# Latent attention block: VectorE and ScalarE in program order in blocks 1 to 3, with new buffer pools, piece places and load order

## The chip, the cores and the metric

The kernel runs on one core of a Trainium2 chip. The time is the device time of one execution in microseconds (us); the median of several executions is given. Lower is better.

## The reference

One transformer block on 2048 tokens of width 512, batch 1: latent attention with 16 heads, a residual and a layer norm, then one linear layer, a residual and a second layer norm.

```python
cq  = rms_norm(x @ w_qa.T, q_a_ln_w)                  # query latents, width 384
q   = cq @ w_qb.T                                     # 16 heads of 128 + 64
ckv = x @ w_kva.T                                     # width 128 + 64
ckv_l = rms_norm(ckv[..., :128], kv_a_ln_w)
kv  = ckv_l @ w_kvb.T                                 # 16 heads of 128 (keys) + 128 (values)
# rotary embedding on the 64-wide parts of q and of ckv
scores = einsum('bhqd,bhkd->bhqk', q_full, k_full) * 192 ** -0.5
scores = where(causal, -inf, scores)
out = softmax(scores) @ v                             # per head
x = layernorm(x + out @ w_o.T)
x = layernorm(x + x @ (w * scale_weight[:, None]).T + bias)
```

The result must be close to float32, so most operands are kept as a high and a low half, and each product is made of three products of halves.

## The kernel before

The key projection is folded into the query weights and the value projection into the output weights, so that all heads share one set of keys (`Kn`, `Kp`) and values (`V`). The 2048 queries are cut into four blocks `b` of 512. A block runs over eight pairs `p` of heads, a pair over four query tiles `qt` of 128 rows, and from block 1 on each tile over its two heads `j`. One such (b, p, qt, j) is called a head here; blocks 1 to 3 have 64 each. It has `nk` = (4b + qt + 1) x 128 keys: 640 to 1024 in block 1, 1152 to 1536 in block 2, 1664 to 2048 in block 3. Block 0 handles both heads of a tile at once, interleaved with the projections of the inputs and the weights. After block 3 a tail multiplies by the output weights, adds, normalizes and runs the linear layer (L763 onward is its layer norm, L786 its largest product).

The work on one head, in the order in which the program emits it:

- `head_scores`: TensorE writes the scores into PSUM (L408), in one piece `s` up to 1024 keys and in two beyond. There are three score buffers in blocks 1 and 3; block 2 has two for the first piece and two smaller ones for the second. VectorE adds the causal mask to the last 128 keys (L414; in block 3 for j = 0, TensorE does it at L410), and takes the maximum of each piece (L441). Between the two pieces' maxima the generator of the head before is advanced. A small operation makes the exponential's bias (L448 for one piece, L450 for two). The rest of the head before follows. ScalarE then takes the exponential into `pr` (L456), with its sum, and VectorE inverts the sum (L466 or L468, then L469).
- `head_probs`, a generator that is run while the next head is being emitted: ScalarE writes the scaled probabilities as float16 into `hl` (L477), VectorE writes what float16 left over (L480), both in two cuts from 1152 keys on; then one DMA transposes `hl` into the ring `PT` (L484), issued from SP.
- `values`: TensorE multiplies the transposed probabilities of a pair of heads by `V` (L533), in two halves that are run some heads later (`run_values`, with a lag of three query tiles in blocks 1 and 2 and two in block 3); ScalarE copies the result to `ot` (L538), and it goes to memory.
- `fill` advances the projections for the next pair or block by one piece of nine matmuls, at the heads whose number 2 qt + j is listed in `at`. `project_nope` has two pieces, each followed by L66 on ScalarE and L67 on VectorE. `project_pe`, once in two pairs, has two pieces as well, each followed by two L339 on VectorE; after the second, GpSimd combines the products (L346, L347), ScalarE rounds them (L349), and GpSimd spreads them (L360, L361).

The order of TensorE and of SP is the program's own in blocks 1 to 3 (`manual_schedule`). VectorE, ScalarE and GpSimd are ordered by a scheduler that works from its own estimate of durations. All pools of blocks 1 to 3 are one pool `blk13` with two buffers for each of `pr` and `hl`, and the ring lies in it. `load_wq` and `load_block`, called at the end of the last pair's query projection, put the loads of the next block's query weights `wq`, of its query latents `cq` (1.5 MB) and of its rotary tables `cs` on SP's queue.

Of the kernel before, what the change touches and what calls it, by code (L numbers as in the profile page):

```python
# [9 lines left out]
F16 = mybir.dt.float16  # L10
BF16 = mybir.dt.bfloat16
F32 = mybir.dt.float32
# [7 lines left out]
P = 128  # L20
# [5 lines left out]
NB = 4  # L26
QB = 512
NPAIR = H // 2
# [21 lines left out]
def mla_block(ctx: ExitStack, tc: tile.TileContext, a, out):  # L50
# [6 lines left out]
    def move(queue, dst, src):  # L57
        queue.dma_start(dst.bitcast(F32), src.bitcast(F32))

    def split(ps, h, l, scale=None):  # L60

        if scale is None:
            nc.scalar.activation(h, ps, AF.Copy)  # L63
            nc.vector.tensor_tensor(l, ps, h.bitcast(F32), ALU.subtract)  # L64
        else:
            nc.scalar.activation(h, ps, AF.Copy, scale=scale)  # L66
            nc.vector.scalar_tensor_tensor(l, ps, scale, h.bitcast(F32), ALU.mult, ALU.subtract)  # L67
# [42 lines left out]
    blk = ctx.enter_context(tc.tile_pool(name="blk", bufs=2, side="right"))  # L110
# [177 lines left out]
    def put_in(all=False):  # L288
        kept = []
        for n, dst, src in later:  # L290
            if n == 0 or all:
                nc.sync.dma_start(dst, src)
            else:
                kept.append([n - 1, dst, src])
        later[:] = kept

    def load_block(b):
        if b == NB:
            return
        cq = prj.tile([P, 2, LT, QB], F32R, tag="cq", name=f"cq{b}")  # L300
        if b:
            move(state["queue"], cq, cq_d[b])
        cs = prj.tile([P, 2, QB], F32, tag="cs", name=f"cs{b}")
        (state["queue"] if b else nc.sync).dma_start(cs, a["csq"][b])
        state["cq"], state["cs"] = cq, cs
# [3 lines left out]
    def load_wq(b, p):  # L309
        if b == NB:  # L310
            return
        w = state["wq", b, p] = prj.tile([P, 2, LT, 256], F32R, tag="wq", name=f"wq{b}_{p}")
        c0 = (p % 2) * 256
        move(state["queue"], w, wq_d[p // 2][:, :, :, c0 : c0 + 256])
# [52 lines left out]
    def project_nope(b, p, direct=None):  # L367
        if direct is None and ("wq", b, p) not in state:
            load_wq(b, p)
        w = state.pop(("wq", b, p)) if direct is None else direct  # L370
        cq = state["cq"]
        qn = blk.tile([P, 2, 2, QB], F32R, tag="qn", name=f"qn{b}_{p}")
        for j in range(2):
            ps = psum["m"].tile([P, QB], F32, tag="m", name=f"ps_qn{b}_{p}_{j}")
            n = 0
            for lt in range(LT):
                for i, k in ((0, 0), (0, 1), (1, 0)):
                    nc.tensor.matmul(  # L378
                        ps, w[:, i, lt, j * P : (j + 1) * P], cq[:, k, lt, :], start=n == 0, stop=n == 8
                    )  # L380
                    n += 1
            split(ps, qn[:, 0, j, :], qn[:, 1, j, :], kvln)
            if j == 1:
                state["qn", b, p] = qn
                if b or p == NPAIR - 1:
                    load_wq(*((b, p + 1) if p + 1 < NPAIR else (b + 1, 0)))
                if p == NPAIR - 1:
                    load_block(b + 1)
            yield

    def project(b, p):
# [27 lines left out]
    def head_scores(pool, b, p, j, qt, nk, prev):  # L419
        t = 4 * b + qt  # L420
        r = rq[:, t : t + 1]
        cks = chunks(nk)
        nt = len(cks)
        neg = small.tile([P, 2], F32, tag="neg", name="neg")
        tiles = []
        for ti, ck in enumerate(cks):

            if b == 2 and ti == 1:
                ps = psum["t"].tile([P, 1, 512], F32, tag="t", name=f"s{b}_{p}_{qt}_{j}_{ti}", bufs=2)
            else:  # L430
                ps = psum["s"].tile(
                    [P, 2, 512], F32, tag="s", name=f"s{b}_{p}_{qt}_{j}_{ti}", bufs=2 if b == 2 else 3
                )
            w = ck[0][1]
            for ci, (c0, w) in enumerate(ck):
                d = nk - P - c0
                score(ps[:, ci, :], c0, w, b, p, j, qt, d if 0 <= d < w else None)
            v = ps[:, : len(ck), :w]
            if ti == nt - 1 == 0:
                next(prev, None)  # L440
            nc.vector.tensor_reduce(neg[:, ti : ti + 1], v, axis=AX.XY, op=ALU.max, negate=True)  # L441
            tiles.append((v, ck[0][0], len(ck), w))
            if ti < nt - 1:
                next(prev, None)
                next(prev, None)
        bias = small.tile([P, 1], F32, tag="bias", name="bias")
        if nt == 1:
            nc.vector.tensor_scalar(bias, neg[:, 0:1], r, None, ALU.mult)  # L448
        else:
            nc.vector.tensor_scalar(bias, neg[:, 0:1], neg[:, 1:2], r, ALU.min, ALU.mult)  # L450
        for _ in prev:
            pass
        pr = pool.tile([P, nk], F32, tag="pr", name=f"pr{b}_{p}_{qt}_{j}")
        sums = small.tile([P, 2], F32, tag="sums", name="sums")
        for ti, (v, c0, n, w) in enumerate(tiles):
            nc.scalar.activation(  # L456
                pr[:, c0 : c0 + n * w].rearrange("p (a c) -> p a c", a=n),
                v,
                AF.Exp,
                bias=bias,  # L460
                scale=r,
                accum_out=sums[:, ti : ti + 1],
            )
        inv = small.tile([P, 1], F32, tag="inv", name="inv")
        if nt == 1:
            nc.vector.tensor_scalar(inv, sums[:, 0:1], 1.0 / P_UP, None, ALU.mult)  # L466
        else:
            nc.vector.tensor_scalar(inv, sums[:, 0:1], sums[:, 1:2], 1.0 / P_UP, ALU.add, ALU.mult)  # L468
        nc.vector.reciprocal(inv, inv)  # L469
        return pr, inv  # L470

    def head_probs(pool, b, p, j, qt, nk, PT, pr, inv):
        hl = pool.tile([P, 2, nk], F16, tag="hl", name=f"hl{b}_{p}_{qt}_{j}")
        step = nk if nk <= 1024 else nk // 2
        cuts = [slice(c, c + step) for c in range(0, nk, step)]
        for c in cuts:
            nc.scalar.activation(hl[:, 0, c], pr[:, c], AF.Copy, scale=inv)  # L477
        yield
        for c in cuts:
            nc.vector.scalar_tensor_tensor(hl[:, 1, c], pr[:, c], inv, hl[:, 0, c], ALU.mult, ALU.subtract)  # L480
            if c != cuts[-1]:
                yield
        n2 = 2 * nk
        nc.sync.dma_start_transpose(  # L484
            PT[:, j * n2 : (j + 1) * n2].rearrange("p (k q) -> p k q", q=P), hl.rearrange("p a c -> p (a c)")
        )
        put_in()
# [64 lines left out]
    def drain():  # L552
        while fillers:
            fill()
# [48 lines left out]
    def flush():  # L603
        while probs:
            for _ in probs.pop():
                pass

    def units(pool, ring, b):
        lag = min(ring.shape[1] // (2048 * (b + 1)) - 1, 3)

        for p in range(NPAIR):
# [1 line left out]


            if p + 1 == NPAIR:
                at = (1, 2, 4, 5) if b < NB - 1 else (1, 3, 5, 7)
            elif p % 2 == 0 and p + 2 < NPAIR:
                at = (0, 1, 2, 3) if (b, p) == (1, 0) else (0, 1, 3, 4)
            else:
                at = (3, 4)  # L620
            if b and p % 2 == 0 and p + 2 < NPAIR:
                fillers.append(project_pe(b, p // 2 + 1))
            if p + 1 < NPAIR:
# [24 lines left out]
            for qt in range(4):  # L648
                nk = (4 * b + qt + 1) * P
# [28 lines left out]
                        run_values(lag)  # L678
                vals.append([vg, 0, s0, s0 + 4 * nk])
            drain()  # L680

    def half_values():
        next(vals[0][0])
# [37 lines left out]

    ctx_m = ctx.enter_context(ExitStack())
    psum["m"] = ctx_m.enter_context(tc.tile_pool(name="ps_m", bufs=2, space=PSUM, side="right", reuse_waits="tile"))
    blk13 = ctx_m.enter_context(tc.tile_pool(name="blk13", bufs=2, reuse_waits="tile"))
    ring = blk13.tile([P, 12 * 2048], F16, name="ring", bufs=1)
    side[:] = []
    state["queue"] = nc.sync
    with tc.manual_schedule(engines={mybir.EngineType.PE, mybir.EngineType.SP}):
        for b in range(1, NB):
            with ExitStack() as ctx_s:  # L730
                for k in ("t", "s") if b == 2 else "s":
                    psum[k] = ctx_s.enter_context(
                        tc.tile_pool(name=f"ps_{k}{b}", bufs=1, space=PSUM, reuse_waits="tile")
                    )
                units(blk13, ring, b)
        put_in(True)
    state["queue"] = nc.gpsimd
    pcr, wvo, wv, wo = (state[k] for k in ("pcr", "wvo", "wv", "wo"))
# [89 lines left out]
            if late and next(late[0], None) is None:  # L828
                late.pop(0)

    ET = mybir.EngineType
    CUT = 2
    with tc.manual_schedule(engines={ET.PE}):
        order = [(b, p) for b in range(NB) for p in range(NPAIR)]
# [93 lines left out]
```

## Time and profile before

| | us |
|---|---|
| median of 3 executions (1647.24 to 1654.08) | 1650.19 |
| the profiled execution | 1647.43 |
| its span | 1645.3 |
| block 0, with all projections of the inputs (to the first scores of block 1) | 257.5 |
| block 1, 64 heads | 254.0 |
| block 2, 64 heads | 360.9 |
| block 3, 64 heads | 501.6 |
| last values and tail | 271 |

The profile's names: PE is TensorE's matmuls and PEld its weight loads, DVE is VectorE, ACT ScalarE, POOL GpSimd, SP the engine that issues most DMAs. A group's row gives line, engine, operation, what it writes and reads, the shape, its count, busy time, the mean duration of one, and, behind the last bar, the idle time of the engine before it and what ended that. In the order of time a row begins with its start and duration in us, and a bracket gives the idle time of that engine before it and the releaser. A row of windows gives the stretch, its length, the busy time and count of each engine, the granted clock of TensorE as a share of full speed, the busy share of the DMA engines and GB/s.

Waits that the other sections refer to, from the list of waits (engine and line that waited, what it waited for; total us, times, longest): VectorE's inv (L468) for the exponential (L456) 78.2, 64, 2.4; ScalarE's exponential for the bias (L450) 110.6, 69, 5.6; ScalarE's L477 for the transposing DMA 69.8, 40, 6.8; TensorE's scores for the exponential 26.5, 25, 3.6; TensorE's L334 for the query latents 4.5, 2, 3.1.

### The profile page before, as it was taken

The page shows a single profiled execution, that of the slowest core. Times are in us where ns is not written, and L with a number is a line of the kernel's source. Part 1 is how long each engine was busy: PE and PEld are TensorE (multiplying, and loading weights), DVE is VectorE, ACT ScalarE, POOL GpSimd, SP SyncE. Part 2 cuts the span into 40 slices and gives each one's busy share as a digit, 9 for nine tenths or more (in the row PEclk, how much of TensorE's full clock was granted, in tenths as well). Part 3 has the DMA queues.
Part 4 walks back from the last instruction along what each step waited for, and adds up shares of the span by engine and source line. Part 5 has one row for each costly group of instructions (what it writes and reads, how often), then busy time and mean ns, then how long its engine had stood idle before and what let it go on. Part 6 is the DMA issues. An engine that isn't in the chain of part 4 may idle for free. (4 is left out here: it accounts for less than half of the span.)

```text
span 1645.3 us, 24717 instructions
## 1 busy us (share of the span) xinstructions
PE 1563.1 (95%) x9130; PEld 1295.0 (79%) x9130; DVE 1162.4 (71%) x2099; ACT 928.4 (56%) x1631; POOL 361.7 (22%) x436
## 2 busy tenths in 40 slices
PE   8898999999999999999999999999998997999997
PEld 7787877888777888888887787787786785788876
DVE  5778678787768888888786777777776673555564
ACT  4777766665646676667665666666665563311120
POOL 2342426045016213050053103103100000022132
PEclk9999999999999999999999999999999999999999
DMA  6889666888888888788986787786788788333230
GB/s 208 237 225 236 174 179 159 153 170 170 148 188 172 163 171 166 152 167 159 201 168 144 141 162 139 155 161 126 149 161 175 161 173 187 104 115 120 98 109 32
DMA packets 632839, 262.48 MB, mean 160 GB/s; under 512 B 570288, under 2 KB 611120, under 8 KB 631696
## 3 DMA queue, kind: packets, MB, share of 16 engines
q1 hardware_dynamic: 621184, 233.35, 66.2%
q0 software_dynamic: 4768, 17.99, 3.5%
q10 hardware_dynamic: 6768, 9.57, 2.1%
q8 instruction: 72, 1.18, 0.3%
q14 instruction: 47, 0.39, 0.1%
HBM read 83.17 MB, written 35.13 MB: 72 GB/s over the span
## 5 line engine op out<-in xcount | busy, mean ns | idle before, releaser
L408 PE MATMUL s<-Kn,qn 128*128 128x512 f32 (+4 forms) x1920 | 524.6, 379 | 28.4 <-ACT pr L456 26.5
L533 PE MATMUL o<-ring,V 128*128 128x256 f16 x3252 | 397.0, 275 | 19.4 <-DMA ring<-hl 14.8
L456 ACT ACTIVATE pr<-s,bias,rq 128x1024 f32<-128x1024 f32 (+3 forms) x320 | 324.1, 1016 | 150.8 <-DVE bias L450 110.6
L408 PEld LDWEIGHTS s<-Kn,qn 128*128 128x128 f32 x1920 | 339.7, 191 | 82.6 <-ACT pr L456 38.7
L480 DVE SCALAR_TENSOR_TENSOR hl<-pr,inv,hl 128x1024 f16<-128x1024 f32 (+7 forms) x320 | 357.2, 1137 | 66.1 <-ACT hl L477 64.6
L477 ACT ACTIVATE hl<-pr,inv 128x1024 f16<-128x1024 f32 (+7 forms) x320 | 295.4, 961 | 172.5 <-DMA ring<-hl 69.8
L533 PEld LDWEIGHTS <-V 128*128 128x128 f16 x3264 | 304.4, 98 | 101.2 <-issue 54.6
L441 DVE TENSOR_REDUCE neg<-s 128x1 f32<-128x1024 f32 (+3 forms) x320 | 318.6, 996 | 75.4 <-PE s L408 71.0
L408 PE MATMUL s<-Kp,pe 128*128 128x512 f32 (+4 forms) x1280 | 363.0, 365 | 0.0
L408 PEld LDWEIGHTS s<-Kp,pe 128*128 128x128 f32 x1280 | 235.3, 190 | 29.8
L346 POOL TENSOR_TENSOR prod<-prod 128x512 f32<-128x512 f32 x15 | 19.2, 1283 | 666.6 <-DVE prod L339 666.6
L378 PE MATMUL ps_qn<-cq,wq 128*128 128x512 f32 x576 | 145.9, 398 | 0.7 <-ACT ot L538 0.3
L361 POOL TENSOR_TENSOR pe<-prod,ph 32x512 fp32r<-32x512 f32 x92 | 141.6, 1539 | 11.0 <-issue 5.1
L786 PE MATMUL acc<-wvo,oh 128*128 128x512 f32 x448 | 143.5, 401 | 0.0
L378 PEld LDWEIGHTS ps_qn<-cq,wq 128*128 128x128 f32 x576 | 107.9, 191 | 22.1 <-ACT ot L538 0.8
L786 PEld LDWEIGHTS acc<-wvo,oh 128*128 128x128 f32 x448 | 83.4, 188 | 20.9 <-issue 2.9
L284 POOL DMA_DIRECT2D ot_d<-ot x33 | 18.8, 568 | 319.2 <-ACT ot L538 292.3
L786 PE MATMUL acc<-wvo,ol 128*128 128x512 f32 x224 | 88.4, 394 | 0.0
L468 DVE TENSOR_SCALAR inv<-sums 128x1 f32<-128x1 f32 x128 | 26.9, 210 | 78.3 <-ACT pr L456 78.2
L538 ACT ACTIVATE ot<-o 128x256 f32<-128x256 f32 x128 | 48.0, 376 | 59.9 <-PE o L533 59.9
L334 PE MATMUL ps_pe<-cq,wpe 128*128 128x512 f32 x288 | 71.9, 395 | 5.6 <-DMA cq<-cq_d 4.5
L66 ACT ACTIVATE qn<-ps_qn,kvln 128x512 fp32r<-128x512 f32 x64 | 43.7, 684 | 51.1 <-PE ps_qn L378 51.0
(140 smaller groups left out, 1608.8 us busy)
## 6 DMA issues: line engine op xcount, KB each, us to landing
wq<-wq_d SPq DMA_DIRECT2D x22, 768.0 KB, 5.7
o<-ot_d SPq DMA_DIRECT2D x32, 512.0 KB, 3.3
ot_d<-ot SPq DMA_DIRECT2D x95, 128.0 KB, 2.6
wpe<-wpe_d SPq DMA_DIRECT2D x10, 768.0 KB, 5.3
wq<-wq_d POOLq DMA_DIRECT2D x9, 768.0 KB, 6.4
wq_d<-wst SPq DMA_DIRECT2D x9, 512.0 KB, 4.4
cq_d<-cqst SPq DMA_DIRECT2D x18, 256.0 KB, 3.8
ot_d<-ot POOLq DMA_DIRECT2D x33, 128.0 KB, 3.2
```

The lines of the kernel that those rows point to most:

```text
L66: nc.scalar.activation(h, ps, AF.Copy, scale=scale)
L334: nc.tensor.matmul(ps, w[:, i, lt, x * P : (x + 1) * P], cq[:, k, lt, :], start=n == 0, stop=n == 8)
L361: (nc.gpsimd if not quick or (b, g) == (0, 0) and j % 2 else nc.vector).tensor_tensor(pe[64 + 32 * x : 96 + 32 * x, j, :], rp[q, x, :], ph ...
L378: nc.tensor.matmul(ps, w[:, i, lt, j * P : (j + 1) * P], cq[:, k, lt, :], start=n == 0, stop=n == 8)
L408: nc.tensor.matmul(ps[:, :w], lhs, K[:, i, c0 : c0 + w], start=n == 0, stop=n == 4)
L441: nc.vector.tensor_reduce(neg[:, ti : ti + 1], v, axis=AX.XY, op=ALU.max, negate=True)
L456: nc.scalar.activation(pr[:, c0 : c0 + n * w].rearrange("p (a c) -> p a c", a=n), v, AF.Exp, bias=bias, scale=r, accum_out=sums[:, ti : ti ...
L477: nc.scalar.activation(hl[:, 0, c], pr[:, c], AF.Copy, scale=inv)
L480: nc.vector.scalar_tensor_tensor(hl[:, 1, c], pr[:, c], inv, hl[:, 0, c], ALU.mult, ALU.subtract)
L533: nc.tensor.matmul(ps[:, :256], vt[:, i, k % 4, :], v[:, :, l, k, :], start=n == 0, stop=n == 3 * kts - 1)
L538: nc.scalar.activation(ot, ps[:, :256], AF.Copy)
L786: nc.tensor.matmul(acc, l[:, t, c], wvo[p][:, i, j, :], start=p == 0 and j == 0 and n == 0, stop=p == NPAIR - 1 and j == 1 and n == 2,)
```

## The change

Five edits, in one step:

1. In blocks 1 to 3 VectorE and ScalarE too run in the order in which the program emits their instructions. Instructions from outside these blocks may still be placed among them by the scheduler.
2. Each block gets a pool of its own for `pr` and `hl`; the ring gets another. `hl` has 6, 4 and 2 buffers in blocks 1, 2 and 3, `pr` has 4, 2 and 2. At the end of a block the last head's generator is run out (`flush`), since its pool is closed.
3. The places of the projection pieces, `at`, move: two heads apart in most pairs.
4. At the end of the last pair's query projection the loads of `cq` and `cs` come before that of `wq`.
5. `ET` is defined earlier; nothing else hangs on it.

```diff
             if j == 1:
                 state["qn", b, p] = qn
+                if p == NPAIR - 1:
+                    load_block(b + 1)
                 if b or p == NPAIR - 1:
                     load_wq(*((b, p + 1) if p + 1 < NPAIR else (b + 1, 0)))
-                if p == NPAIR - 1:
-                    load_block(b + 1)
...
-        pr = pool.tile([P, nk], F32, tag="pr", name=f"pr{b}_{p}_{qt}_{j}")
+        pr = pool.tile([P, nk], F32, tag="pr", name=f"pr{b}_{p}_{qt}_{j}", bufs=4 if b == 1 else 2)
...
-        hl = pool.tile([P, 2, nk], F16, tag="hl", name=f"hl{b}_{p}_{qt}_{j}")
+        hl = pool.tile([P, 2, nk], F16, tag="hl", name=f"hl{b}_{p}_{qt}_{j}", bufs=(6, 4, 2)[b - 1])
...
             if p + 1 == NPAIR:
-                at = (1, 2, 4, 5) if b < NB - 1 else (1, 3, 5, 7)
-            elif p % 2 == 0 and p + 2 < NPAIR:
-                at = (0, 1, 2, 3) if (b, p) == (1, 0) else (0, 1, 3, 4)
+                at = (1, 2, 4, 6) if b < NB - 1 else (1, 3, 5, 7)
+            elif p + 2 == NPAIR:
+                at = (1, 3)
+            elif p % 2 == 0:
+                at = (0, 1, 2, 4) if (b, p) == (1, 0) else (0, 2, 4, 6)
             else:
-                at = (3, 4)
+                at = (3, 5)
...
             drain()
+        if b:
+            flush()
...
-    blk13 = ctx_m.enter_context(tc.tile_pool(name="blk13", bufs=2, reuse_waits="tile"))
-    ring = blk13.tile([P, 12 * 2048], F16, name="ring", bufs=1)
+    ring = ctx_m.enter_context(tc.tile_pool(name="rings", bufs=1, reuse_waits="tile")).tile(
+        [P, 12 * 2048], F16, name="ring"
+    )
...
-    with tc.manual_schedule(engines={mybir.EngineType.PE, mybir.EngineType.SP}):
+    ET = mybir.EngineType
+    with tc.manual_schedule(engines={ET.PE, ET.SP, ET.DVE, ET.Activation}):
...
-                units(blk13, ring, b)
+                blkb = ctx_s.enter_context(tc.tile_pool(name=f"blk{b}", bufs=2, reuse_waits="tile"))
+                units(blkb, ring, b)
```

More of the change, by code (lines that the diff above doesn't have):

```diff
@@ L829, in advance @@
                 late.pop(0)
-    ET = mybir.EngineType
     CUT = 2
```

## The prediction, made before the changed kernel was run

> **What bounds the kernel now.** I read the busy shares first, then the three attention blocks as windows, then the waits, then the order of instructions inside a block. The profiled execution took 1647.43 us (span 1645.3, 2.1 us around it), 2.8 below the median of 1650.19; sums are made against it and 2.8 is added at the end.
>
> ```profile
> PE 1563.1 (95%) x9130; PEld 1295.0 (79%) x9130; DVE 1162.4 (71%) x2099; ACT 928.4 (56%) x1631; POOL 361.7 (22%) x436
> ...
> 257.50:511.50 254.00, 240.34 (x1431) 202.52 (x1429) 198.41 (x414) 150.89 (x241) 83.95 (x74) 0.99 0.81 164
> 511.50:872.40 360.90, 355.52 (x2149) 299.52 (x2149) 291.15 (x548) 244.06 (x439) 83.64 (x72) 0.99 0.84 168
> 872.40:1374.00 501.60, 483.77 (x2900) 396.28 (x2901) 353.80 (x511) 301.80 (x437) 61.56 (x54) 0.99 0.78 153
> ```
>
> The windows are blocks 1, 2 and 3 (64 heads of work each; columns: PE, PEld, DVE, ACT, POOL busy). TensorE idles 13.7, 5.4 and 17.8 us in them: 37 us is nearly all that any reordering here can win. In block 2 TensorE needs 355.5 / 64 = 5.55 us a head; that number is the yardstick below.
>
> The gaps of TensorE have three kinds:
>
> ```profile
> 447.10 1.15 ACT L477 ACTIVATE hl<-pr,inv 128x1024 f16<-128x1024 f32 x1 [2.59 <-DMA ring<-hl]
> 450.89 0.95 PE L408 MATMUL s<-Kn,qn 128*128 128x384 f32 x3 [1.24 <-ACT pr L456]
> ...
> 480.02 2.32 PE L334 MATMUL ps_pe<-cq,wpe 128*128 128x512 f32 x9 [3.12 <-DMA cq<-cq_d]
> ...
> 997.62 2.47 DVE L480 SCALAR_TENSOR_TENSOR hl<-pr,inv,hl 128x1024 f16<-128x1024 f32 x2
> 1000.01 0.27 DVE L450 TENSOR_SCALAR bias<-neg,rq 128x1 f32<-128x1 f32 x1
> 1001.66 0.71 PE L408 MATMUL s<-Kn,qn 128*128 128x320 f32 x3 [0.91 <-ACT pr L456]
> ```
>
> In block 1 ScalarE waits for one of two hl buffers, and the exponentials (L456) behind it keep score PSUM occupied. At 480 the query latents are late. In block 3 both cuts of the residual (L480) run ahead of the bias (L450), so the exponential is 2.5 us late.
>
> **The change, part by part.**
>
> *hl and pr buffers per block (hl 6, 4, 2; pr 4, 2, 2).* The ten gaps of block 1 at pair ends add up to 7.4 us, with 1.7 more for a half-clock window behind one. They go; block 3 keeps two buffers, and loses nothing.
>
> *Query latents first.* The built program issues cq before cs and wq, and about one head (4 us) earlier, so the 768 KB of wq no longer precede it. The 3.1 us gap at 480 and the 1.4 at 238 go (the latter is outside these blocks). wq is wanted two pieces later; its transfer takes 5.7 us to land (issue rows), a head takes 4, so it is covered. SP issues the same three transfers ahead of the same transposes.
>
> *Program order on VectorE and ScalarE.* This closes a loop. In block 2, before:
>
> ```profile
> 668.85 0.16 DVE L469 RECIPROCAL inv<-inv 128x1 f32<-128x1 f32 x1
> 669.03 1.22 DVE L441 TENSOR_REDUCE neg<-s 128x1 f32<-128x1024 f32 x1
> ...
> 672.42 0.27 DVE L450 TENSOR_SCALAR bias<-neg,rq 128x1 f32<-128x1 f32 x1
> ...
> 672.73 1.20 ACT L456 ACTIVATE pr<-s,bias,rq 128x1024 f32<-128x1024 f32 x1
> 674.71 0.21 DVE L468 TENSOR_SCALAR inv<-sums 128x1 f32<-128x1 f32 x1 [1.26 <-ACT pr L456]
> 674.96 0.17 DVE L469 RECIPROCAL inv<-inv 128x1 f32<-128x1 f32 x1
> 676.29 1.23 DVE L441 TENSOR_REDUCE neg<-s 128x1 f32<-128x1024 f32 x1 [1.17 <-PE s L408]
> 677.43 0.94 DVE L480 SCALAR_TENSOR_TENSOR hl<-pr,inv,hl 128x704 f16<-128x704 f32 x1
> 678.29 0.29 DVE L414 TENSOR_TENSOR s<-s,maskb 128x128 f32<-128x128 f32 x1
> 679.35 0.55 DVE L441 TENSOR_REDUCE neg<-s 128x1 f32<-128x384 f32 x1
> 679.94 0.27 DVE L450 TENSOR_SCALAR bias<-neg,rq 128x1 f32<-128x1 f32 x1
> ```
>
> Elsewhere in block 2 the scheduler ran the next head's first maximum (L441) beside the current exponential. In the built changed program every head reads on VectorE: inv, reciprocal, first maximum of the next head, first L480 cut of this one, mask, second maximum, bias, second cut. The maximum now queues behind inv, which waits for the exponential, which waits for the bias. Only the second cut runs beside the exponential. From start to start at 1408 keys: bias to exponential 0.31, to inv 1.98, to reciprocal 0.25, to maximum 0.18, to L480 1.14, to mask 0.86, to second maximum 0.34 (a mask of 0.29 and the hand-over), to bias 0.59: 5.65 us. Exchanging the durations of the shapes (exponential of 256, 384, 512 columns 0.55, 0.66, 0.77; second maximum 0.42, 0.55, 0.69; 0.98 and 0.95 in place of 1.20 and 1.22 for 768) gives 5.05, 5.35, 5.65, 5.95 for 1152 to 1536 keys, mean 5.50, x64 = 352. TensorE has 4.8 a head without a projection piece (355.5 less 24 pieces of 2.1).
>
> Onto this loop come, in program order between reciprocal and maximum: 8 times two L339 (2 x 0.64 less overlap, 1.2): 10; 16 times L67, which waits for L66 (0.69) behind the exponential: 0.95 each, 15. L480's mean in the rows by shape is 0.12 above its quiet 0.78 to 0.98 where GpSimd is busy; I count half, 4. And 4 times L349: it now stands on ScalarE before this head's L477, and waits for two L339 and two GpSimd operations of 1.3, about 3.9 us behind the exponential; L477, then the L480 that VectorE waits at, are 3.0 us late: 12. Sum 352 + 10 + 15 + 4 + 12 = 393 against 360.9: **+32**. Two heads of score buffers let TensorE run ahead but do not open the loop.
>
> Here a rule of the Trainium skill speaks against me: "Perfetto Trace Analysis", section "Identifying the Most-Contended Engine", looks for the engine of highest occupancy. In block 2 that is PE (355.5 of 360.9), VectorE has 291; by it, a VectorE order costs nothing and the block takes some 357. The row at 674.71, VectorE idle 1.26 us for the exponential, says that a waiting engine below full share can pace; I take the rows, and keep the rule's 357 for the range.
>
> Block 1, same sum: 2.85, 3.09, 3.33, 3.57 for 640 to 1024 keys, mean 3.21, x64 = 205; L339 10, L67 17, L349 4 x 2.7 = 11: 243 against TensorE's 240. Three score buffers smooth it; with mutual waits 247 for 254: **-7** (between -14, TensorE alone, and 0).
>
> Block 3: 6.12 to 7.07, mean 6.59, x64 = 422; with 33 for L339, L67 and L349: 455, below TensorE's 484. So TensorE paces, the bias is no longer behind both cuts, and 9.9 us of gaps at pair ends go. *Pieces two heads apart* moves one to the second head of pair 6, where a 4.5 us gap at 1267 waits for transposes behind 2 MB of wv and wo: 2.1 of it are covered. The L349 stall exceeds the 1.5 us of slack (4.8 us of TensorE work before it needs the tile, 3.3 of mask to exponential) by about 1, three times. **-9**. The gaps at 872 (3.6), 1301 (3.5; the built program still puts two of the tail's L64 between maximum and bias) and 1390 (8.3, last transposes) stay.
>
> The clock is the second place. Mean granted clock stands before DMA share and GB/s:
>
> ```profile
> 447.50:451.00 3.50, 1.75 (x13) 1.06 (x12) 2.67 (x4) 3.03 (x5) 0.00 (x0) 1.00 0.32 84
> 451.00:454.80 3.80, 3.80 (x13) 3.61 (x14) 2.19 (x10) 1.79 (x3) 0.00 (x0) 0.55 1.05 211
> ```
>
> "TensorE: Matmul & The Clock Gate", Part 1, puts the return to half clock after one idle window of about 3.4 us. Here 1.75 idle of 3.5 sufficed. By the rule, waits of 3 us at L349 cost no clock; by the row each costs 1.7 us, 7 in block 2. I add none, since TensorE would not pace there, and keep 7 for the range.
>
> Sum: -1.4 - 7 + 32 - 9 = +15: 1662 in a profile, **1665** as median.
>
> **Rivals.**
> - *Faster:* TensorE stays the bound in block 2 because the loop stays below its 5.55 us a head. For it: VectorE was never over 81% busy; against: the 5.65 read above, before any piece. Then -1.4 - 11 - 4 - 9 = -25, a median of 1625. It decides from the loop: below 375 us for block 2 (5.9 a head) the whole is faster.
> - *Slower still:* the L349 hold drains the score buffers in all blocks, and TensorE restarts at half clock: 11 stalls of 3 us less slack plus 1.7, some 25 more: 1690. Against: block 1 has three heads of buffers.
> - *A wash:* block 2 costs only the bare loop and its pieces (352 + 25 = 377), gains as summed: 1650. The tail's instructions still stand inside block 3, so program order is not complete there; that is the part that does not do what it says.
>
> **How the numbers follow.** Forecast (1655 to 1680) 0.58; faster 0.23; wash 0.10; slower still 0.09. About 0.5% (8 us) is what a measurement can tell. Slower takes the forecast's case but 0.02, and the last rival: 0.65; same 0.11; faster 0.24. The range 1628 to 1688 takes in the rule's bound for block 2 partly, and the clock.
>
> **What would show it.** Block 2 near 393 us with TensorE about 90% busy, VectorE's idle time before inv (now 78.2 us in all) well up, and TensorE's waits for L456 spread over all of block 2; block 1 near 247 with no ScalarE wait for ring<-hl; block 3 near 493; no wait for cq. Block 2 at 360 or less would refute the loop.

## The result, and the profile after

The changed kernel takes 1659.20 us (median of 5 runs, 1658.72 to 1660.72), the kernel before 1650.19 beside it (median of 5 as well, 1647.24 to 1654.08): ratio 1.0052, interval 1.0037 to 1.0068. It is slower by 9 us, half a percent. The profiled span is 1657.4 us against 1645.3; the profiled execution of the kernel before was 2.8 us below its median, so the blocks differ by 12 us in all and not by 9. By blocks, each from the first scores of a block to those of the next, block 3 to its last bias:

| us | before | after | difference | predicted |
|---|---|---|---|---|
| block 0 | 257.5 | 259.0 | +1.5 | -1.4 (latents) |
| block 1 | 254.0 | 249.6 | -4.4 | -7 |
| block 2 | 360.9 | 397.5 | +36.6 | +32 |
| block 3 | 501.6 | 479.7 | -21.9 | -9 |
| last values and tail | 271.3 | 271.6 | +0.3 | 0 |

The windows of blocks 1, 2 and 3 of the changed kernel (columns as before: PE, PEld, DVE, ACT, POOL busy, then granted clock, DMA share, GB/s):

```profile
259.00:508.60 249.60, 238.91 (x1433) 201.88 (x1430) 208.59 (x420) 156.10 (x247) 80.25 (x73) 0.99 0.81 168
508.60:906.10 397.50, 364.99 (x2151) 303.64 (x2148) 296.14 (x548) 245.38 (x439) 85.67 (x74) 0.97 0.74 153
906.10:1385.80 479.70, 475.90 (x2894) 394.42 (x2895) 357.09 (x510) 298.02 (x435) 64.30 (x54) 1.00 0.81 160
```

In block 2 TensorE now stands still for 32.5 us (397.50 less 364.99; before 5.4), although it is still the fullest engine: VectorE is busy 296 of 397 us. In block 3 it stands still for 3.8 us where it was 17.8. Which wait carries this shows in the costliest groups of instructions of the page (busy, mean ns, then the idle time just before and what ended it):

```profile
L456 ACT ACTIVATE pr<-s,bias,rq 128x1024 f32<-128x1024 f32 (+3 forms) x320 | 325.4, 1021 | 321.6 <-DVE bias L450 259.4
L533 PE MATMUL o<-ring,V 128*128 128x256 f16 x3252 | 399.9, 276 | 37.4 <-ACT ot L538 24.4
L468 DVE TENSOR_SCALAR inv<-sums 128x1 f32<-128x1 f32 x128 | 27.4, 214 | 162.2 <-ACT pr L456 162.2
```

VectorE waits for the exponential (162.2 us, before 78.2), and the exponential waits for VectorE's bias (259.4, before 110.6). These are sums over the whole kernel. In block 2 alone the waits of the changed kernel are (us in total, times, longest):

```profile
ACT pr L456 <- DVE bias L450: 113.7, 61, 3.4
DVE inv L468 <- ACT pr L456: 76.3, 63, 1.9
PE o L533 <- ACT ot L538: 20.4, 11, 4.4
```

Before, the first two were 23.4 and 15.1 us there. Two engines that wait for each other in turn, neither of them full, are a closed loop. Here is one turn of it in block 2, VectorE alone, in order of time:

```profile
694.69 0.27 DVE L450 TENSOR_SCALAR bias<-neg,rq 128x1 f32<-128x1 f32 x1
694.88 0.94 DVE L480 SCALAR_TENSOR_TENSOR hl<-pr,inv,hl 128x704 f16<-128x704 f32 x1
697.04 0.21 DVE L468 TENSOR_SCALAR inv<-sums 128x1 f32<-128x1 f32 x1 [1.22 <-ACT pr L456]
697.29 0.16 DVE L469 RECIPROCAL inv<-inv 128x1 f32<-128x1 f32 x1
697.62 0.75 DVE L67 SCALAR_TENSOR_TENSOR qn<-ps_qn,kvln,qn 128x512 fp32r<-128x512 f32 x1 [0.17 <-ACT qn L66]
698.29 1.22 DVE L441 TENSOR_REDUCE neg<-s 128x1 f32<-128x1024 f32 x1
699.42 0.94 DVE L480 SCALAR_TENSOR_TENSOR hl<-pr,inv,hl 128x704 f16<-128x704 f32 x1
700.28 0.29 DVE L414 TENSOR_TENSOR s<-s,maskb 128x128 f32<-128x128 f32 x1
700.61 0.69 DVE L441 TENSOR_REDUCE neg<-s 128x1 f32<-128x512 f32 x1
701.34 0.27 DVE L450 TENSOR_SCALAR bias<-neg,rq 128x1 f32<-128x1 f32 x1
```

Everything between `inv` and the next bias waits for the exponential of this head, and only the second cut of L480 (694.88) runs beside it. The turn before this one, without a piece and also at 1408 keys, took 5.58 us from exponential to exponential (689.48 to 695.06); this one 6.65 (695.06 to 701.71), 0.13 of it because the second maximum is wider.

### The profile page after: what moved, and what is told of

It is laid out like the page before. It is cut to its first block, busy times and chain, and to the rows that moved or that the text cites. A ratio compares the mean times of both kernels' runs of the same rounds, so it can differ in the third digit from the quotient of the medians.

```text
span 1657.4 us, 24735 instructions
## 1 busy us (share of the span) xinstructions
PE 1565.7 (94%) x9130; PEld 1298.8 (78%) x9130; DVE 1179.2 (71%) x2099; ACT 929.8 (56%) x1631; POOL 364.6 (22%) x436
## 5 line engine op out<-in xcount | busy, mean ns | idle before, releaser
L456 ACT ACTIVATE pr<-s,bias,rq 128x1024 f32<-128x1024 f32 (+3 forms) x320 | 325.4, 1021 | 321.6 <-DVE bias L450 259.4
L533 PE MATMUL o<-ring,V 128*128 128x256 f16 x3252 | 399.9, 276 | 37.4 <-ACT ot L538 24.4
L533 PEld LDWEIGHTS <-V 128*128 128x128 f16 x3264 | 307.2, 99 | 121.6 <-issue 76.9
L480 DVE SCALAR_TENSOR_TENSOR hl<-pr,inv,hl 128x1024 f16<-128x1024 f32 (+7 forms) x320 | 360.4, 1127 | 36.9 <-ACT hl L477 34.5
L477 ACT ACTIVATE hl<-pr,inv 128x1024 f16<-128x1024 f32 (+7 forms) x320 | 295.7, 963 | 59.7 <-ACT pr L456 31.4
L346 POOL TENSOR_TENSOR prod<-prod 128x512 f32<-128x512 f32 x15 | 19.3, 1284 | 700.3 <-DVE prod L339 700.3
L361 POOL TENSOR_TENSOR pe<-prod,ph 32x512 fp32r<-32x512 f32 x92 | 141.4, 1537 | 11.0 <-issue 5.1
L468 DVE TENSOR_SCALAR inv<-sums 128x1 f32<-128x1 f32 x128 | 27.4, 214 | 162.2 <-ACT pr L456 162.2
L334 PE MATMUL ps_pe<-cq,wpe 128*128 128x512 f32 x288 | 74.4, 405 | 6.5 <-DMA cq<-cq_d 3.8
L334 PEld LDWEIGHTS ps_pe<-cq,wpe 128*128 128x128 f32 x288 | 54.5, 194 | 17.4 <-DMA cq<-cq_d 4.0
L64 DVE TENSOR_TENSOR ol<-o,oh 128x1024 fp32r<-128x1024 f32 x28 | 38.6, 1378 | 40.8 <-ACT oh L63 40.8
```

The costliest lines, as they stand in the source:

```text
L334: nc.tensor.matmul(ps, w[:, i, lt, x * P : (x + 1) * P], cq[:, k, lt, :], start=n == 0, stop=n == 8)
L361: (nc.gpsimd if not quick or (b, g) == (0, 0) and j % 2 else nc.vector).tensor_tensor(pe[64 + 32 * x : 96 + 32 * x, j, :], rp[q, x, :], ph ...
L456: nc.scalar.activation(pr[:, c0 : c0 + n * w].rearrange("p (a c) -> p a c", a=n), v, AF.Exp, bias=bias, scale=r, accum_out=sums[:, ti : ti ...
L533: nc.tensor.matmul(ps[:, :256], vt[:, i, k % 4, :], v[:, :, l, k, :], start=n == 0, stop=n == 3 * kts - 1)
```

## The experiments

All are variants of the changed kernel unless said otherwise. Times are medians in us. The ratio is to the kernel before, run beside each group of variants (its medians were 1646.2 to 1650.2), so variants of different groups are better compared by their ratios than by their medians. The blocks are those of one profiled execution each; block 0, which no edit but that of the load order touches, lies between 256.3 and 263.2 in them, so a few us in a whole can come from there.

| | median | ratio, interval | block 0 | 1 | 2 | 3 |
|---|---|---|---|---|---|---|
| changed kernel | 1659.2 | 1.0052 (1.0037 to 1.0068) | 259.0 | 249.6 | 397.5 | 479.7 |
| VectorE and ScalarE scheduled again | 1634.7 | 0.990 (0.9857 to 0.9943) | 256.3 | 244.8 | 366.7 | 495.2 |
| VectorE in program order only | 1643.6 | 0.9955 (0.9938 to 0.9973) | 259.5 | 240.3 | 392.6 | 479.2 |
| ScalarE in program order only | 1642.1 | 0.9946 (0.9928 to 0.9964) | 256.9 | 255.6 | 364.8 | 491.8 |
| kernel before, with the order alone | 1686.6 | 1.0208 (1.0152 to 1.0264) | 263.2 | 263.6 | 405.2 | 480.4 |
| two buffers of hl and pr | 1682.3 | 1.0191 (1.0165 to 1.0217) | 256.7 | 269.8 | 402.2 | 479.0 |
| places of the pieces as before | 1666.3 | 1.0107 (1.0074 to 1.0140) | 258.4 | 250.8 | 400.2 | 480.1 |
| wq loaded first, as before | 1657.6 | 1.0066 (1.0043 to 1.0088) | 259.8 | 246.3 | 397.2 | 480.7 |
| second maximum of block 2 twice | 1698.5 | 1.031 (1.0279 to 1.0341) | 258.2 | 249.6 | 437.0 | 480.3 |
| rounding L349 on GpSimd | 1646.9 | 0.9978 (0.9964 to 0.9991) | 261.1 | 246.0 | 390.2 | 477.8 |
| first cut of L480 after the bias | 1617.5 | 0.9796 (0.9754 to 0.9838) | 261.4 | 249.5 | 358.9 | 474.2 |
| the last two together | 1611.5 | 0.9780 (0.9747 to 0.9813) | 262.4 | 246.5 | 357.0 | 474.0 |
| the last, and wq loaded first | 1605.4 | 0.9728 (0.9712 to 0.9745) | 259.7 | 242.4 | 356.8 | 473.9 |

**The order taken back, and the order alone.** The first leaves the pools, the places and the loads as changed:

```diff
-    with tc.manual_schedule(engines={ET.PE, ET.SP, ET.DVE, ET.Activation}):
+    with tc.manual_schedule(engines={ET.PE, ET.SP}):
```

> The changed kernel with VectorE and ScalarE given back to the scheduler; pools, piece places and load order stay. Loop theory (program order closes a loop over VectorE and ScalarE that paces block 2): block 2 returns from 397 us to 355 to 368, block 3 goes back up from 480 to 490 to 502 since both L480 cuts may stand before the bias again, block 1 stays at 240 to 250; the whole 1630 to 1650. Rival (the new pools, places or loads cost the time in block 2): block 2 stays above 385 us, the whole above 1655.

The second gives the kernel before the new set of engines and nothing else:

```diff
-    with tc.manual_schedule(engines={mybir.EngineType.PE, mybir.EngineType.SP}):
+    with tc.manual_schedule(engines={mybir.EngineType.PE, mybir.EngineType.SP, mybir.EngineType.DVE, mybir.EngineType.Activation}):
```

> The kernel before with VectorE and ScalarE in program order and nothing else changed. Loop theory: block 2 takes 390 to 405 us, block 3 478 to 490, block 1 255 to 270 because ScalarE now stands in order behind a wait for one of two hl buffers; the whole 1665 to 1685. Rival (pools and places cost the time): block 2 stays within 361 to 372 us.

Without the order block 2 falls from 397.5 to 366.7, and with the order alone it rises from 360.9 to 405.2: the slowdown belongs to the order. The rest of the change, without it, makes the kernel 1% faster. With the order alone block 1 too grew, from 254.0 to 263.6, as was expected with two hl buffers. The whole came out 1.6 us above its range; block 0, to which the expectation gave nothing, was 5.7 us longer.

**Which of the two engines.** Each is put in program order by itself:

```diff
-    with tc.manual_schedule(engines={ET.PE, ET.SP, ET.DVE, ET.Activation}):
+    with tc.manual_schedule(engines={ET.PE, ET.SP, ET.DVE}):
```

> The changed kernel with ScalarE again ordered by the scheduler in blocks 1 to 3; VectorE stays in program order. Theory (it is VectorE's order, with the next first maximum behind the inverse of the sum, that closes the loop; ScalarE's order adds only the hold at L349, some 7 to 12 us in block 2): block 2 at 383 to 397, the whole 1642 to 1660. Rival (ScalarE's order, where L477 and the copies L538 stand between exponentials, is what paces): block 2 at 370 or less, the whole below 1635.

```diff
-    with tc.manual_schedule(engines={ET.PE, ET.SP, ET.DVE, ET.Activation}):
+    with tc.manual_schedule(engines={ET.PE, ET.SP, ET.Activation}):
```

> The changed kernel with VectorE again ordered by the scheduler in blocks 1 to 3; ScalarE stays in program order. In the built order most first maxima of block 2 stand ahead of the inverse of the sum, or one cut of L480 behind the bias. Theory (VectorE's order makes the loop): block 2 at 360 to 376 (TensorE's 355 and the hold at L349), the whole 1630 to 1645. Rival (ScalarE's order paces by itself): block 2 at 385 or more, the whole 1650 or more.

The window of block 2 with VectorE in order alone:

```profile
499.70:892.30 392.60, 363.57 (x2151) 300.60 (x2148) 302.86 (x547) 246.86 (x438) 88.18 (x75) 0.99 0.76 154
```

and with ScalarE in order alone:

```profile
512.40:877.20 364.80, 354.75 (x2151) 298.40 (x2149) 297.42 (x547) 241.65 (x439) 86.28 (x73) 1.00 0.84 167
```

VectorE's order makes the loop; ScalarE's does not. Taken in steps from the kernel before, block 2 is: the rest of the change +5.8 (360.9 to 366.7), VectorE's order +25.9 (to 392.6), ScalarE's on top +4.9 (to 397.5). Block 1: -9.2, -4.5, then +9.3 for ScalarE's order. Block 3: -6.4, -16.0, +0.5. With ScalarE's order taken first, its steps in blocks 1 to 3 are +10.8, -1.9 and -3.4, and VectorE's after it -6.0, +32.7 and -12.1. In either sequence VectorE's order is the loss in block 2 and the gain in block 3, and ScalarE's costs some 10 us in block 1 and is small elsewhere. The rest of the change has no fixed price in block 2: under the scheduler it adds 5.8 us, which was not followed up, but on top of the order it saves 7.7 (405.2 to 397.5).

**Does VectorE's work come out whole?** If a loop paces, work put into it lengthens the block by as much:

```diff
             nc.vector.tensor_reduce(neg[:, ti : ti + 1], v, axis=AX.XY, op=ALU.max, negate=True)
+            if b == 2 and ti == 1:
+                nc.vector.tensor_reduce(neg[:, ti : ti + 1], v, axis=AX.XY, op=ALU.max, negate=True)
```

> The changed kernel with VectorE's second maximum (0.42 to 0.69 us, by its columns) done twice in each of the 64 heads of block 2, nothing else. Theory (VectorE's and ScalarE's closed loop paces block 2, so every microsecond put on it comes out whole): block 2 longer by 64 x 0.57 = 36 us, within 30 to 40, about 434, the whole 1690 to 1700. Rival (TensorE, or the score buffers with two heads of slack, pace most of block 2 and VectorE, busy 75% of it, has room for 0.6 us a head): block 2 longer by less than 15 us, the whole below 1675. Between, 15 to 30: the loop paces only part of the heads.

The window of block 2 in that kernel:

```profile
507.80:944.80 437.00, 375.36 (x2151) 309.10 (x2148) 335.99 (x612) 245.22 (x439) 82.65 (x74) 0.95 0.68 140
```

VectorE has 64 more instructions (612 for 548) and 39.9 us more of busy time (335.99 less 296.14); the block is 39.5 us longer. An engine busy 75% of a stage passed on 99% of what was added to it.

**Opening the loop.** One of the two steps of the previous head's generator between the two maxima is left to after the bias. The first cut of L480 then no longer stands before the second maximum, and both cuts run beside the exponential:

```diff
             if ti < nt - 1:
                 next(prev, None)
-                next(prev, None)
```

> The changed kernel with one line less: between the two maxima the head before is advanced once instead of twice, so that its first L480 cut goes behind the bias with the second and leaves the loop. Loop theory: the loop of block 2 falls by 0.86 us a head to about 4.8, with pieces 5.4 to 5.5, under TensorE's 5.55: block 2 takes 358 to 372 us (from 397), block 3 475 to 482, block 1 unchanged; the whole 1620 to 1635. Rival (L349, which holds ScalarE, or the wait of L533 for L538 sets block 2): less than 12 us are won.

The list of waits of that whole kernel (us in total, times, longest; its lines from 445 on stand one lower):

```profile
DVE neg L441 <- PE s L408: 80.0, 93, 2.4
...
DVE inv L467 <- ACT pr L455: 39.5, 94, 2.3
```

VectorE now waits for TensorE's scores (80.0 us, after the change 18.0) and far less for the exponential (39.5, was 162.2); in block 2 alone 17.6 for the scores, after the change 0.2, and 20.5 for the exponential, was 76.3. TensorE paces block 2 again, 358.9 us with 353.9 busy, and the gain in block 3 stays. The whole is 2.5 us below the range expected.

**The hold at L349.** The rounding goes to GpSimd, which makes its input anyway, except in the first pair of block 1 and before it:

```diff
-        nc.scalar.activation(ph, rp, AF.Copy)
+        if (b, g) > (1, 0):
+            nc.gpsimd.tensor_copy(ph, rp)
+        else:
+            nc.scalar.activation(ph, rp, AF.Copy)
```

> The changed kernel with the rounding L349 moved from ScalarE to GpSimd in blocks 1 to 3 (from the second group on), so that ScalarE no longer waits about 3.9 us for GpSimd in front of L477. Loop theory with L349 as a term of 12 us of it in block 2: block 2 from 397 to 382 to 390, blocks 1 and 3 0 to 4 us shorter each, the whole 1642 to 1652. Rival (L349 is the cause and not the loop): block 2 at 370 or below. Second rival (its hold is hidden by the score buffers): within 3 us of 397.

The hold in the changed kernel, ScalarE in order of time:

```profile
632.26 1.06 ACT L349 ACTIVATE ph<-prod 128x1024 fp32r<-128x1024 f32 x1 [3.85 <-POOL prod L347]
633.23 1.53 ACT L477 ACTIVATE hl<-pr,inv 128x640 f16<-128x640 f32 x2
636.48 1.21 ACT L456 ACTIVATE pr<-s,bias,rq 128x1024 f32<-128x1024 f32 x1 [1.72 <-DVE bias L450]
```

The wait is as predicted, 3.85 us, but taking it away gains only 7.3 us in block 2 (12 were put down for it) and 3.6 in block 1. VectorE's rows say why. In the changed kernel:

```profile
634.07 1.33 DVE L480 SCALAR_TENSOR_TENSOR hl<-pr,inv,hl 128x640 f16<-128x640 f32 x1 [2.90 <-ACT hl L477]
639.81 1.83 DVE L480 SCALAR_TENSOR_TENSOR hl<-pr,inv,hl 128x640 f16<-128x640 f32 x1
```

and with the rounding on GpSimd (this line is L483 there):

```profile
627.51 1.83 DVE L483 SCALAR_TENSOR_TENSOR hl<-pr,inv,hl 128x640 f16<-128x640 f32 x1
640.28 1.60 DVE L483 SCALAR_TENSOR_TENSOR hl<-pr,inv,hl 128x704 f16<-128x704 f32 x1
646.51 1.92 DVE L483 SCALAR_TENSOR_TENSOR hl<-pr,inv,hl 128x704 f16<-128x704 f32 x1
```

The wait for L477, 2.6 to 2.9 us at each of the four holds of block 2, is gone. But where an operation of these widths otherwise takes 0.87 to 0.96 us, two are long in the first stretch and three in the second. From exponential to exponential, the turns around a hold, less their L339 and L67, are 4.5 us longer than bare turns in the first kernel and 2.8 in the second; four times the difference is 7 us. All five long ones run while GpSimd works on these products (L346 to L361, 629.6 to 651.3 in the first kernel); others beside them do not grow, and that GpSimd's work is the cause was not shown by a run.

With the edit of the cut as well (both are shown in part):

```diff
-                next(prev, None)
...
+        if (b, g) > (1, 0):
+            nc.gpsimd.tensor_copy(ph, rp)
```

> The changed kernel with two edits together: one of the two steps of the previous head's generator between the two maxima is left to after the bias, so that one cut of L480 no longer stands before the second maximum, and the rounding L349 goes from ScalarE to GpSimd from the second pair of block 1 on. Alone they gave 1617.5 and 1646.9. Theory (with the first edit TensorE paces block 2 again, so the hold of ScalarE at L349 lies beside it): the second edit adds 0 to 4 us of gain, 1613 to 1618, block 2 at 356 to 359. Rival (the two gains add, as the loop still paces): 1604 to 1609, block 2 about 351 or less, which is below TensorE's own 355 and would need fewer half-clock stretches. Second rival (GpSimd's rounding lengthens the L480 beside it[...]): 1619 or more.

Block 2 is at 357.0: once TensorE paces, most of the hold lies beside its work. The whole, 1611.5, lies between what the theory and its rival expected. The ratios of this kernel and of the one with the first edit alone overlap, so the whole does not tell the second edit from nothing; by the blocks it gains 1.9 us in block 2 and 3.0 in block 1.

**The buffers.**

```diff
-        pr = pool.tile([P, nk], F32, tag="pr", name=f"pr{b}_{p}_{qt}_{j}", bufs=4 if b == 1 else 2)
+        pr = pool.tile([P, nk], F32, tag="pr", name=f"pr{b}_{p}_{qt}_{j}", bufs=2)
...
-        hl = pool.tile([P, 2, nk], F16, tag="hl", name=f"hl{b}_{p}_{qt}_{j}", bufs=(6, 4, 2)[b - 1])
+        hl = pool.tile([P, 2, nk], F16, tag="hl", name=f"hl{b}_{p}_{qt}_{j}", bufs=2)
```

> The changed kernel with two buffers each for hl and pr in all three blocks, as before the change; pools, places, order and loads stay changed. Theory (the buffers matter in block 1 alone, where ScalarE's L477 waits for a transposing DMA that still holds one of two hl; the loop of block 2 hangs on VectorE's order, not on buffers): block 1 longer by 8 to 14 us (258 to 264), TensorE's gaps at pair ends back, block 2 within 5 us of 397, block 3 as it is, the whole 1667 to 1676. Rival (with ScalarE in program order the waits for hl cost nothing in block 1, and the changed places of the pieces are what shortened it): block 1 within 3 us of 250, the whole 1657 to 1662.

Block 1 takes 269.8, more than either theory had, 20 us above the changed kernel; block 2 is 4.7 longer too, and the whole is above both ranges. The list of waits of the whole kernel has the reason:

```profile
ACT hl L477 <- DMA ring<-hl: 48.8, 30, 6.8
```

In the changed kernel this wait is 6.3 us in all. Of the 48.8, 35.0 lie in block 1. The kernel before waited longer there, 43.5 us, and yet took only 254.0; the order alone, which changes nothing but the order, waits 31.2 there and takes 263.6. So a wait for a buffer costs more under program order. The likely reason, argued from the order of the program, is that the next exponential stands behind the waiting L477. The buffers are what makes the order bearable in block 1.

**The places.** `at` as in the kernel before:

```diff
             if p + 1 == NPAIR:
-                at = (1, 2, 4, 6) if b < NB - 1 else (1, 3, 5, 7)
-            elif p + 2 == NPAIR:
-                at = (1, 3)
-            elif p % 2 == 0:
-                at = (0, 1, 2, 4) if (b, p) == (1, 0) else (0, 2, 4, 6)
+                at = (1, 2, 4, 5) if b < NB - 1 else (1, 3, 5, 7)
+            elif p % 2 == 0 and p + 2 < NPAIR:
+                at = (0, 1, 2, 3) if (b, p) == (1, 0) else (0, 1, 3, 4)
             else:
-                at = (3, 5)
+                at = (3, 4)
```

> The changed kernel with the places of the projection pieces (`at`) of before. Theory (the places matter only in block 3, where one piece moved to the second head of pair 6 fills a wait for the transposing DMA, and in block 2 each piece's L67 or L339 is paid by VectorE's loop wherever it stands): block 2 within 4 us of 397, block 3 longer by 2 to 6 us with TensorE's wait of about 4.5 us near 1280 back, the whole 1658 to 1667. Rival (pieces next to each other overfill single heads, so spreading them two heads apart is what kept block 3 and block 1 short): block 3 longer by 10 us or more, block 1 by 4 or more, the whole 1670 or more. Second rival (the spread costs in block 2, as each piece interrupts another head): block 2 shorter by 8 us or more, the whole about 1650.

Block 3 does not move (480.1), so the gain there is not the places'; TensorE's wait near 1290 is 1.8 us, not 4.5. Block 2 is 2.7 longer. The four runs lie between 1661.3 and 1669.1, and the profiled one is the fastest of them, so the blocks show only part of it. By the ratios, whose intervals do not touch, the new places gain about 9 us over the old ones, by the medians 7.

**The loads.**

```diff
-                if p == NPAIR - 1:
-                    load_block(b + 1)
                 if b or p == NPAIR - 1:
                     load_wq(*((b, p + 1) if p + 1 < NPAIR else (b + 1, 0)))
+                if p == NPAIR - 1:
+                    load_block(b + 1)
```

> The changed kernel with one edit taken back: at the end of a block the next block's wq is again loaded before cq and cs. Theory (the load order is what removed the 3.1 us wait of TensorE's L334 at the start of block 2's query work, and it moved 768 KB of wq behind the latents, which may be why the first L334 of block 1's queries now waits 3.8 us near 237 us where it waited 1.4): the wait at about 475 us comes back with some 3 us, the one at 237 falls to 1 to 2 us, and the whole moves by less than 3 us against the changed kernel, 1656 to 1662. Rival (the latents' order has nothing to do with either wait, block 0's own ordering by the scheduler sets the one at 237): 3 to 4 us stay at 237, and the whole is slower by the 3 us at 475, 1660 to 1664. Loop theory: block 2 stays at 390 to 400 in either case.

TensorE's two first L334 of a new block, with wq loaded first:

```profile
240.22 2.33 PE L334 MATMUL ps_pe<-cq,wpe 128*128 128x512 f32 x9 [1.41 <-DMA cq<-cq_d]
...
478.00 2.24 PE L334 MATMUL ps_pe<-cq,wpe 128*128 128x512 f32 x9
```

and in the changed kernel the first of them:

```profile
236.94 3.92 PE L334 MATMUL ps_pe<-cq,wpe 128*128 128x512 f32 x9 [3.77 <-DMA cq<-cq_d]
```

Half of each theory fell. The wait of 3.1 us before block 2 does not come back with the old load order, nor with the old places and the new load order. It is not there with the order alone either, which has the old places and the old load order: its latents are issued at 479.4 us, land 9.3 us later, and TensorE comes to them at 490.6, where the kernel before issued them at 468.8, they landed after 11.1 us, and TensorE came to them at 476.9. So program order by itself is enough to remove this wait. At the end of block 0, which the scheduler orders, the wait is longer with latents first, but no later: TensorE is ready for L334 at 233.2 in place of 238.8, and starts it at 236.9 in place of 240.2. The medians differ by 1.6 us one way and the ratios by 0.14% the other, with intervals that overlap: the load order alone is not told from nothing. With the two edits that open the loop the load order does count:

> The version with one cut of L480 after the bias and the rounding on GpSimd (1611.5), and wq again loaded before cq and cs. Theory (either the load order or the earlier place of the query piece is enough for the latents of block 2; the load order gains nothing at all): the whole within 3 us of 1611.5, blocks 0 and 1 together within 3 us of 509, no wait for cq near 475. Rival (the latents' order costs at the end of block 0, as the run with it taken back was 2.5 us shorter over blocks 0 and 1): 1607 to 1609.

1605.4 is 6 us below the same kernel with latents first, more than the rival gave, all of it in blocks 0 and 1 (502.1 against 508.9); the intervals of the two ratios only just do not touch. What in those blocks the load order moves, beyond the place of L334, stays open; the scheduler's order of block 0 changes with every edit here. It is the fastest version, 2.7% below the kernel before, with TensorE busy 354.0 of 356.9 us in block 2 and 472.3 of 473.9 in block 3.

## Why the prediction was right, and where it was not

The whole, 1665 forecast and 1659.2 measured, is closer than its parts: blocks 0 to 2 came out 10 us longer than forecast, block 3 came out 13 shorter, and the 2.8 us added for the median were not there. That these nearly cancel is luck. The mechanism is not.

**The loop** was the reason given, and it is the reason shown. Four kinds of runs say so: the order alone makes it, VectorE's order without ScalarE's makes it, work added to VectorE passes through at 0.99, and moving one L480 cut out of it gives block 2 back to TensorE. The bare turn was put at 5.65 us and is 5.58; a head with L67 was to cost 0.95 more and costs 0.94 (6.65 less 5.58 less 0.13).

**The sum for block 2** had 393 and measured 397.5, and its terms can be read from the changed kernel's trace, from exponential to exponential of the 64 heads (517.17 to 913.20, 396.0 us):

| term | forecast | read |
|---|---|---|
| bare turns, 64 | 352 | 351 (5.10 to 5.91 each) |
| two L339, 8 times | 10 | 9 |
| L67, 16 times | 15 | 15 (0.93 each) |
| hold at L349, and L480 beside GpSimd, 4 times | 12 + 4 | 18 (4.5 each) |
| last turn, at the change to block 3 | none | 3.4 |

The terms are nearly right one by one, and the sum did not come out by luck. What it had no term for is the change of blocks: the last turn takes 9.17 us where the last turns of the other pairs take 5.78, and TensorE waits 5.7 us for block 3's first scores, where 3.6 stood before and was said to stay. The window is 1.5 us longer than the 64 turns, since it begins and ends with scores.

**Block 1** (-7, measured -4.4): the gaps at pair ends went, as said, but the step "three score buffers smooth it" was too kind to ScalarE's order. VectorE's order alone reaches 240.3, ScalarE's adds 9.3. TensorE still stands still for 10.7 us (before 13.7), now in part for ScalarE's copies L538 and once 2.1 us for L339.

**Block 3** (-9, measured -21.9) is the largest error. The mechanism was named (both cuts of L480 no longer ahead of the bias at pair ends), and a term was mis-sized: I took off the 9.9 us of gaps at pair ends and 2.1 of the wait at 1267, gave 3 back for the hold at L349, and left "TensorE's 484" as fixed work. The idle time fell by 14.0, since waits that I let stand went too (all of the 4.5 at 1267, and the 3.5 at 1301 is now 1.1), and the busy time of the same matmuls fell by 7.9 (483.77 to 475.90). Of that, 4.4 are half-clock stretches, which before stood behind the waits at 872, 1267 and 1301 (windows of 3 us, their length times one less the granted clock: 6.2 before, 1.8 after); the other 3.5 are not explained. A busy time that holds half-clock stretches is not a floor. Taking the hold at L349 away, for which I charged block 3 some 3 us, gave back 1.9 there (rounding on GpSimd).

**Query latents first** (-1.4 with the 3.1 in block 1): wrong in its cause for the one wait, which is gone without this edit too, and in its sign for the other, which grew from 1.4 to 3.8 us, as the runs with the load order taken back and with the order alone show.

**The rule against the row.** From the rule of the Trainium skill ("Perfetto Trace Analysis", section "Identifying the Most-Contended Engine") that the engine of highest occupancy is the one to look at, I had drawn some 357 us for block 2. The section would have TensorE judged by its weight loads rather than by its matmuls; they were busy 299.5 of 360.9 us there, 83%, so TensorE came first by them too, but hardly ahead of VectorE's 81%. The row of a waiting VectorE gave 393, and the row was right: VectorE's share fell from 81% to 75% while it came to set the pace.

On the clock, the row of the kernel before (half clock after 1.75 us of idle time in 3.5) does not agree with the one idle window of about 3.4 us in the Trainium skill, "TensorE: Matmul & The Clock Gate", Part 1; the last section has more such rows. The half clock that I kept for the range came, 7.8 us more in block 2 than before, where the row had given 7. Adding none of it to the sum was right as well: the turns of the block are accounted for by VectorE's and ScalarE's rows, as the table of terms shows.

**What was to show it.** Block 2 near 393 with TensorE about 90% busy: 397.5, and 92%. VectorE's idle time before `inv` well up: 162.2. No ScalarE wait for ring<-hl in block 1: none is left there, and 6.3 us in the whole kernel. TensorE's waits for L456 "spread over all of block 2" were not there: in block 2 they fell from 7.9 to 4.1 us, and the idle time stands before L533, for ScalarE's copy L538 of the values before (20.4 us). With VectorE in order alone, at nearly the same length of block 2, the waits of that block read as I had expected:

```profile
PE s L408 <- ACT pr L456: 20.2, 19, 2.0
```

The loop is the same; ScalarE's order decides which of its late products TensorE meets first. The name of a wait is not yet its cause.

## What to carry to other kernels

Before fixing an engine's order, write its instructions between two results of the other engine in a line and add their durations: if an operation behind a wait feeds the next wait, that sum paces the stage where it is longer than the work of the fullest engine (here in block 2, not in block 3), whatever the shares of busy time say. Then move what nothing waits for (here one cut of the residual) behind what the other engine waits for (the bias): one line was worth 42 us here. An order helps one stage and harms another of the same loop, so it is judged stage by stage, and one engine at a time.

## What the runs showed of the hardware

The clock of TensorE falls behind short waits. In the rows of the changed kernel the half clock comes in stretches of 3.41 us or a multiple of it, up to the last, which the end cuts off. Cut into pieces of that length, in step with the half-clock stretches, the trace shows what goes before them. A piece with TensorE's wait behind the hold at L349 and the piece after it, then the same for another wait (columns as before, the granted clock third from the end):

```profile
636.58:639.99 3.41, 1.34 (x13) 1.21 (x13) 2.22 (x5) 3.15 (x7) 3.25 (x4) 1.00 0.51 97
639.99:643.41 3.42, 3.42 (x14) 2.60 (x12) 3.35 (x5) 0.97 (x2) 3.29 (x3) 0.50 0.51 95
...
817.49:820.90 3.41, 1.64 (x16) 1.48 (x15) 2.31 (x5) 3.05 (x8) 0.00 (x0) 1.00 0.84 155
820.90:824.31 3.41, 3.41 (x20) 2.86 (x19) 2.32 (x5) 1.66 (x4) 0.00 (x0) 1.00 0.12 23
```

TensorE was busy for 0.39 of the first piece and half clock followed; it was busy for 0.48 of the third and none did. In this trace every full-clock piece with a share of 0.43 or less was followed by half clock, and of those with 0.47 or more only one was, in the first 25 us. It was this share, and not the length of one wait, that told them apart: a wait of 2.06 us before 864.42 left 0.40 and cost half clock, one of 2.27 before 819.26 left 0.48 and cost none. Over block 2, half clock cost TensorE 10.1 us of speed where it had cost 2.3 before (windows of 3 us, as above), and with the second maximum done twice the mean granted clock of the block fell to 0.95.
